# Two expert blocks of the second mixture layer moved in front of its last routing step, and one choice for the last two sequences

## The chip, the cores and the metric

The kernel runs on one core of a Trainium2 chip. A core has a matrix engine (TensorE, written PE, with its weight loads as PEld), a vector engine (VectorE, DVE), a scalar engine (ScalarE, ACT), a general engine (GpSimd, POOL) and a synchronising engine (SyncE, SP), which issues most transfers. The metric is the time on the device in microseconds (us), lower is better. Everything is computed in float32.

## The reference

The input is 2048 tokens of 128 numbers, as 8 sequences of 256 tokens for the attention. Each of the six sub-layers is added to the stream x:

```python
x = x + 0.5 * ffn(layernorm(x))          # mixture of experts, "layer 1"
x = x + attention(layernorm(x))          # 16 heads of 8, softmax
x = x + 0.5 * ffn(layernorm(x))          # same weights, "layer 2"
x = x + 0.5 * channel_mix(layernorm(x))
x = x + gated_conv(layernorm(x))
x = x + 0.5 * channel_mix(layernorm(x))
```

The mixture of experts has 8 experts, of which each token takes the two with the largest logits:

```python
h = rmsnorm(s @ W_in.T, in_norm_w)                    # 128 -> 128
logits = h @ Wr.T                                     # 8 experts
_, idx = top_k(logits + expert_bias, 2)
gates = softmax(the two logits)
for e in range(8):
    oe = rmsnorm(silu(h @ Wg[e].T) * (h @ Wu[e].T) @ Wd[e].T, enorm_w[e])   # hidden 512
    out = out + gates[:, e] * oe
return rmsnorm(out, out_norm_w) @ W_out.T
```

## The kernel before, in words

A tile is 128 tokens; x is held as four chunks of four tiles. The two mixture layers don't compute all experts for all tokens: each token's row is written to the two places in device memory where the rows of its experts are collected, and the experts then work on blocks of such rows.

`dispatch` (line 338) is the routing for one part of the tiles. Its steps are: `turned` and `measured` (transpose x and take its statistics), `product` (the router's and the input projection, PE, `pin`), `summed` and `inverted` (1/rms: `ri`), `scaled` (the row that is sent, `hrow`, two ACT copies for a tile), `logits`, `choice` twice (first and second expert), `ranked` and `placed` (the row's place among its expert's rows: two products `prank`, and the sums of the tiles before in `ahead`), and `rows` (line 465), two indirect transfers from POOL for a tile, into `hs`. For layer 2 the tiles are cut by `LATE` (line 59) into parts of 4, 4, 4, 2 and 2 tiles. In the first three of layer 2 the 1/rms is POOL's power function (`power_of`, line 170); in layer 1 and in the last two parts of layer 2 it is ACT's square root (line 398) and DVE's reciprocal (line 405).

`counts` (line 492) then has PE sum how many rows each expert has (`pcnt`), and `table` (line 564) works out on DVE, in seven steps (`counted`, `summed`, `paired`, `spared`, `singled`, `named`, `bounded`), which expert and which rows each block takes.

`experts` (line 679) works through blocks. Blocks 24 to 31 are early blocks, one of 128 rows for each expert, whose places are known without the table: their rows are among those of the first tiles (6 tiles in layer 1, 8 in layer 2, `LEAD`) and are read ahead by `leading` (line 517), which also fetches their weights. The others are led by the table: pairs of 256 rows and singles of 128 (numbers 15 and up), in the order of `TURNS` (line 48). For each block i, `work` (line 782) issues: `gate(i)` (eight or four-by-two products `pg`, and ACT's Silu into `sg`), `turn_rows(i+1)` (`pht`, `ht`), `up(i)` (`pu`, and DVE's product `hg`), one step of the table, and `down(i-1)` (`py`, the row's sum of squares `ysq` on ACT, the product with the norm's weights on DVE, two index operations, and one indirect transfer from POOL into `y` for each 128 rows). `py` has one bank of PSUM, so a block's `py` waits until DVE has read the last one. After the last block, `combine` (line 807) reads `y` and adds the two experts of each token.

PE, DVE, ACT and SP execute in the order in which the program issues; POOL's indirect transfers are held in program order too. Attention is a pipeline of steps, and `at(s, h, ...)` puts pieces of layer 2's routing into half-steps of it (lines 1240 to 1300). The last lines of that list bring the last sequences, the rows 0 to 3 of the third part, and the two parts of two tiles each (names ending in 6 and 7, tiles 12 and 13, 14 and 15):

```python
at(33, "a", lead["read"], u6, places, partial(rows, [0]))
at(33, "b", root_table, s6, partial(rows, [1]), w(2))
at(34, "a", partial(turn_back, b), partial(rows, [2]), w(4), i6, l6, c6[0])
at(34, "a", partial(turn_heads, b), partial(rows, [3]), w(2), h6, partial(out_heads, b))
at(34, "a", w(2), x7, w(2), m7, c6[1], u7, w(2), s7, r6)
at(34, "a", i7, p6, rows6, l7, *c7, h7, r7, p7, rows7)
```

`turn_back`, `turn_heads` and `out_heads` are the end of attention for a sequence (`pot`, `pcc`, `ct`, `pwo`, and the addition to x); `w(n)` are n products without use which keep PE busy; `root_table` loads ACT's square root ahead of its use. The expert blocks begin after all of this, in `second_experts` (line 937).

Of the kernel before, what the change touches and what calls it, by code (L numbers as in the profile page):

```python
# [2 lines left out]

# [13 lines left out]
P = 128  # L17
# [28 lines left out]
LEAD = 6, 8  # L46
LEADING = list(range(NT, NT + E))
TURNS = (
    [0, 1, 2, 15, 3, 4, 5, 16, 6, 7, 8, 17, 9, 10, 18, 11],
    [0, 1, 2, 15, 3, 4, 5, 6, 16, 7, 8, 9, 17, 10, 11, 12],  # L50
# [6 lines left out]
EARLY = (0, 4), (4, 4), (8, 4), (12, 4)  # L57
LATE = (0, 4), (4, 4), (8, 4), (12, 2), (14, 2)
# [15 lines left out]
def macaron_kernel(ctx: ExitStack, tc: tile.TileContext, a: dict, out: bass.AP):  # L74
# [70 lines left out]

    root_table()

# [190 lines left out]
    def dispatch(f, i, parts, mp):  # L338
# [5 lines left out]
        paced = f == 1 and i < len(parts) - 2  # L344
# [4 lines left out]
        def turned():  # L349
            pt = bank(f"pxt_{n}", "sa")  # L350
            for t in range(nt):
                nc.tensor.transpose(pt[:, ts(t, P)], x[:, t, :], ident)
            st["xt"] = xntp.tile([P, CT], F32, tag="xnt", name=f"xnt_{n}")
            nc.scalar.copy(st["xt"][:, 0 : nt * P], pt[:, 0 : nt * P])
            st["u"] = mp.tile([P, TPC, D + E], F32, tag="u", name=f"u_{n}")[:, 0:nt]
            st["ss"] = small.tile([P, nt], F32, tag="ss", name=f"ss_{n}")

        def measured():
            bs = small.tile([P, nt, 6], F32, tag="ast", name=f"ast_{n}")
            mv = small.tile([P, nt, 2], F32, tag="amv", name=f"amv_{n}")  # L360
            for t in range(nt):
                nc.vector.bn_stats(bs[:, t, :], x[:, t, :])
            for t in range(nt):
                nc.vector.bn_aggr(mv[:, t, :], bs[:, t, :])
            st["z"] = small.tile([P, nt], F32, tag="z", name=f"z_{n}")
            nc.vector.tensor_scalar(st["z"], mv[:, :, 1], RMS_EPS, RMS_EPS * LN_EPS, ALU.mult, ALU.add)
# [25 lines left out]
        def summed():  # L392
            ri = small.tile([P, nt], F32, tag="ri", name=f"ri_{n}")
            nc.vector.scalar_tensor_tensor(ri, st["ss"], 1.0 / D, st["z"], ALU.mult, ALU.add)
            if f == 0:
                nc.vector.tensor_copy(hrow[:, :, :, D].bitcast(I32), tokid[:, slots])
            if f == 0 or i >= len(parts) - 2:
                nc.scalar.activation(ri, ri, AF.Sqrt)
            else:
                power_of(ri, ri, mhalf.to_broadcast([P, nt]))  # L400
            st["ri"] = ri

        def inverted():
            if f == 0 or i >= len(parts) - 2:
                nc.vector.reciprocal(st["ri"], st["ri"])
# [59 lines left out]
        def rows(ts_=range(nt)):  # L465
            for t in ts_:
                if paced:
                    nc.vector.tensor_copy(st["posi"][:, t, :], st["pos"][:, t, :])
                for k in range(2):
# [5 lines left out]
                    )  # L475
                    tc.declare_no_dep(ins.ins, group=f"hs{f}", reason="rows of their own")
# [11 lines left out]
        if i < len(parts) - 2:  # L488
            return turned, *halves, measured, summed, logits, scaled, *choices, both(ranked, placed), rows
        return turned, halves[0], measured, summed, inverted, logits, scaled, *choices, ranked, placed, rows  # L490

    def counts(f):
        pc = bank(f"pcnt_{f}", "sb")[:, 0:E]
# [22 lines left out]

    def leading(f, gp, homes, rows, yrows):
# [6 lines left out]
        lead["taken"], lead["base"], lead["masks"], lead["idx"] = flags[:, 0], flags[:, 1], masks, idx  # L524

# [19 lines left out]

        def read():
# [5 lines left out]
            for e, row in enumerate(first):  # L552
                hst = rows[e].unsqueeze(1)
# [7 lines left out]
        lead.update(weights=weights, flagged=flagged, read=read)  # L561
# [117 lines left out]
    def experts(f, tab, far, y2, mp, pieces, lead):  # L679
# [3 lines left out]
        hst, w = lead["hst"], lead["w"]  # L683

# [3 lines left out]
        def fetch_weights(t):  # L688
# [3 lines left out]
            e = nc.values_load(tab[0:1, 1, t : t + 1], engines=[SP], min_val=0, max_val=E - 1)  # L692
# [47 lines left out]
        def down(t):  # L740
# [27 lines left out]
            for s in range(m):  # L768
# [10 lines left out]
                if t >= NT:  # L779
                    tc.keep_in_program_order(ins)  # L780
# [961 lines left out]
```

## Time and profile before

| what | us |
|---|---|
| median of three runs (lowest, highest) | 590.76 (589.77, 591.71) |
| the profiled execution's own time | 588.57 |
| its span | 586.8 |
| PE busy | 512.5 (87%) |
| DVE busy | 357.2 (61%) |
| ACT busy | 277.7 (47%) |
| POOL busy | 194.1 (33%) |
| chain that ended last: PE, ACT, DVE, DMA | 64%, 11%, 11%, 9% |
| mean granted PE clock | 0.954 of full speed |

The span holds, one after the other: layer 1's routing (to about 41 us), its early blocks and table blocks (to 154), its combination and the attention (to 354), the end of attention with layer 2's routing of the last tiles and its early blocks (354 to 394), layer 2's table blocks (to 479), and the tail. A row of the timeline gives the start, the busy time, the engine, the line, the operation and its operands, and in square brackets how long the engine stood idle before it and whose work ended the wait. A row of windows gives a stretch with its length and the busy time of each engine in it (with the number of instructions), then the mean clock that PE was granted, the busy share of the DMA engines and the rate in GB/s. In the chain of waits a piece has a start, a length and what it is.

### The profile page before, as it was taken

Reading aid. Unit: us, or ns where it says so; the run is one execution under the profiler, and the core shown is the slowest. Engines: PE = TensorE matmul, PEld = TensorE weight load, DVE = VectorE, ACT = ScalarE, POOL = GpSimd, SP = SyncE. Lnnn points to the kernel's source line nnn. Section 1 sums busy time; section 2 is a strip of 40 time slices with the busy share of each in tenths; the row PEclk is TensorE's granted clock in tenths of the full one; section 3 lists DMA queues with packets and bytes.
Section 4 is the critical chain, followed back from the end, with each engine's and each line's share of the span. In section 5 each row is a group of like instructions: output and inputs, shape, how many; then the busy total and the mean of one; then the engine's idle time right before and its main releaser. Section 6 shows DMA issues by size and latency. Waiting matters only on the chain.

```text
span 586.8 us, 11358 instructions
## 1 busy us (share of the span) xinstructions
PE 512.5 (87%) x3954; PEld 398.6 (68%) x3954; DVE 357.2 (61%) x1129; ACT 277.7 (47%) x683; POOL 194.1 (33%) x202
## 2 busy tenths in 40 slices
PE   5459799999779989998898886989999978799996
PEld 5349788899546555565465554989999945478884
DVE  5777464564336667767768876664444424758775
ACT  4564223222234556566756654433332316874275
POOL 0677546753331201011003356532342335410200
PEclk9559999999989999999999999899999989989998
DMA  8933846765041264073063017455776514000002
GB/s 305 377 91 124 286 159 217 219 185 186 21 109 32 42 165 198 2 203 160 24 127 113 26 36 242 168 173 193 222 224 217 156 45 123 1 1 1 1 0 73
DMA packets 37952, 76.96 MB, mean 131 GB/s; under 512 B 4667, under 2 KB 27106, under 8 KB 36608
## 3 DMA queue, kind: packets, MB, share of 16 engines
q1 hardware_dynamic: 33360, 66.62, 36.3%
q0 software_dynamic: 4528, 9.52, 4.5%
q8 instruction: 35, 0.57, 0.4%
q14 instruction: 29, 0.24, 0.1%
HBM read 55.28 MB, written 21.44 MB: 131 GB/s over the span
## 4 chain that ended last, share of the span: by engine, by line
PE 64%; ACT 11%; DVE 11%; DMA 9%; issue 3%; POOL 1%; SPq 0%; DVEq 0%; ACTq 0%; POOLq 0%
PE pg_f L722 10%; PE pu_f L722 10%; PE ps L1127 9%; PE py_f L745 8%; DMA y<-yrow_f,idx_f 5%; ACT es L1164 4%; PE po L1174 3%; PE pvf L1496 2%; PE pgo L1523 2%; DMA qk<-heads 2%; PE pm L1110 2%; DVE m L1147 2%; PE pin_f L374 1%; PE pk_m L1440 1%; PE pht_f L709 1%
## 5 line engine op out<-in xcount | busy, mean ns | idle before, releaser
L1164 ACT ACTIVATE es<-ps 128x1024 f32<-128x1024 f32 x64 | 65.3, 1021 | 52.9 <-PE ps L1127 31.2
L1147 DVE TENSOR_REDUCE m<-pm 128x4 f32<-128x1024 f32 x64 | 77.4, 1220 | 12.8 <-PE pm L1110 12.7
L1127 PE MATMUL ps<-qa,qk 32*128 32x256 f32 x512 | 73.0, 401 | 11.8 <-ACT es L1164 9.5
L769 POOL DMA_INDIRECT y<-yrow_f,idx_f x57 | 56.0, 983 | 79.3 <-issue 44.3
L470 POOL DMA_INDIRECT hs<-hrow,posi_f x64 | 61.7, 964 | 53.7 <-issue 19.3
L738 DVE TENSOR_TENSOR hg_f<-pu_f,sg_f 128x1024 f32<-128x1024 f32 (+1 forms) x48 | 46.5, 968 | 48.7 <-PE pu_f L722 48.6
L1110 PE MATMUL pm<-qk 32*128 32x256 f32 x512 | 73.8, 401 | 0.9 <-ACT qk L1057 0.6
L762 ACT ACTIVATE ysq_f<-py_f 128x128 f32<-128x128 f32 x73 | 19.7, 274 | 100.2 <-PE py_f L745 91.4
L1127 PEld LDWEIGHTS ps<-qa,qk 32*128 32x128 f32 x512 | 43.6, 184 | 29.7 <-ACT es L1164 22.1
L731 ACT ACTIVATE sg_f<-pg_f 128x1024 f32<-128x1024 f32 (+1 forms) x48 | 39.3, 819 | 44.3 <-PE pg_f L722 42.7
L745 PE MATMUL py_f<-w_f,hg_f 128*128 128x128 f32 x456 | 56.7, 277 | 2.0 <-DVE yrow_f L763 2.0
L745 PEld LDWEIGHTS py_f<-w_f,hg_f 128*128 128x128 f32 x456 | 54.9, 192 | 3.6 <-DVE yrow_f L763 2.3
L722 PE MATMUL pg_f<-ht_f,w_f 128*128 128x256 f32 (+1 forms) x256 | 54.7, 357 | 0.0
L722 PE MATMUL pu_f<-ht_f,w_f 128*128 128x256 f32 (+1 forms) x256 | 54.7, 357 | 0.0
L1110 PEld LDWEIGHTS pm<-qk 32*128 32x128 f32 x512 | 44.6, 184 | 3.3 <-issue 1.5
L722 PEld LDWEIGHTS pu_f<-ht_f,w_f 128*128 128x128 f32 x256 | 43.1, 191 | 4.4
L722 PEld LDWEIGHTS pg_f<-ht_f,w_f 128*128 128x128 f32 x256 | 43.0, 191 | 3.8
L171 POOL TENSOR_TENSOR cf_f<-cf_f,mhalf 128x8 f32<-128x8 f32 (+1 forms) x9 | 13.5, 1503 | 65.8 <-DVE cf_f L834 64.2
L1174 PE MATMUL po<-es,v 128*32 128x256 f32 x512 | 34.3, 385 | 0.0
L763 DVE TENSOR_TENSOR yrow_f<-py_f,w_f 128x256 f32<-128x256 f32 (+1 forms) x32 | 12.7, 396 | 34.6 <-ACT ysq_f L762 32.0
L1159 DVE TENSOR_TENSOR qa<-pmt,qk 128x256 f32<-128x256 f32 x32 | 13.5, 422 | 25.7 <-PE pmt L1153 25.6
L714 DVE TENSOR_SCALAR ht_f<-pht_f,pack 128x256 f32<-128x256 f32 (+1 forms) x32 | 14.5, 453 | 17.3 <-PE pht_f L709 17.3
(327 smaller groups left out, 982.8 us busy)
## 6 DMA issues: line engine op xcount, KB each, us to landing
w_f<-in_wall_dram SPq DMA_DIRECT2D x32, 832.0 KB, 4.6
hs<-blank SPq DMA_DIRECT2D x8, 1032.0 KB, 15.1
qk<-in_wall_dram SPq DMA_DIRECT2D x7, 832.0 KB, 6.5
w_lead<-in_wall_dram SPq DMA_DIRECT2D x7, 832.0 KB, 12.5
y_f<-y SPq DMA_DIRECT2D x14, 258.0 KB, 3.1
hst_f<-hs SPq DMA_DIRECT2D x25, 129.0 KB, 2.2
pack<-in_pack_dram SPq DMA_DIRECT2D x1, 1729.0 KB, 8.5
v<-in_wall_dram SPq DMA_DIRECT2D x2, 832.0 KB
```

Source lines behind the costliest of these rows:

```text
L470: ins = nc.gpsimd.indirect_dma_start(out=hss[f], out_offset=bass.IndirectOffsetOnAxis(ap=st["posi"][:, t, k : k + 1], axis=0), in_=hrow[:, ...
L722: nc.tensor.matmul(ph[:, k, :], w[t][:, o + k * P : o + k * P + P], ht[t], start=True, stop=True)
L731: nc.scalar.activation(sg, pg, AF.Silu)
L738: nc.vector.tensor_mul(hg[t], pu, sg)
L745: nc.tensor.matmul(py[:, s, :], hg[t][:, k, ts(s, P)], w[t][:, 2 * DFF + k * D : 2 * DFF + k * D + D], start=(k == 0), stop=(k == NFC - 1),)
L762: nc.scalar.activation(sq[:, s], py[:, s], AF.Square, accum_out=yrow[:, s, D : D + 1])
L769: ins = nc.gpsimd.indirect_dma_start(out=y2, out_offset=bass.IndirectOffsetOnAxis(ap=idx[:, s : s + 1], axis=0), in_=yrow[:, s, :], in_off ...
L1110: nc.tensor.matmul(sc[:, jj, i, :], qs[c][r, g, col + i * P : col + (i + 1) * P], ks[c][r, g, col : col + S], start=True, stop=True,)
L1127: nc.tensor.matmul(sc[:, jj, i, :], ks[c][r, g, col + i * P : col + (i + 1) * P], tops[s][r, :], start=True, stop=True,)
L1147: nc.vector.tensor_reduce(m, sc, AX.X, ALU.max, negate=True)
L1164: nc.scalar.activation(es, sc, AF.Exp, scale=scale)
L1174: nc.tensor.matmul(po[32 * j : 32 * j + 32, :], vs[c][:, (b % 2) * 2 + i, (g % 2) * (H // 2) + (g // 2) * 4 + j, :], ess[s, j // 2][:, j % ...
```

## The change

- `LATE` and `EARLY` become one `PARTS` of four tiles each: the last two sequences (tiles 12 to 15) are transposed, measured, multiplied and scaled two tiles at a time, but they have one `logits`, one `choice`, one `ranked`, `placed` and `rows`. Their 1/rms goes to POOL's power function, and `silu_table` stands where `root_table` stood in layer 2.
- The blocks 24 and 25 (`BEGUN = 2`) are issued from attention's list, between and behind the steps of that last part: transpositions, gate and up products ahead of and around the routing's `prank`, with smaller tiles of attention's pool and banks of their own; their y rows are sent after the last routing row. `second_experts` begins with block 26.
- The table begins in that list as well: `counts` (now in the bank `sa`), `counted` and `summed`. The remaining steps are spread over the blocks: one for each block in layer 1, with `bounded` in a block of its own; two for each in layer 2.
- In layer 1 the weights of all eight early blocks are asked for at the start (seven before); y rows of the early blocks and the table's scratch move to other buffers. For the first table block the weights are asked for ahead of the rows.
- The index operations of the eight early blocks are done once for all (`numbers`), and for the other blocks ahead of the product with the norm's weights.
- `TURNS`: in layer 1 the single 18 comes after the pair 11, in layer 2 the single 17 after the pair 12.

```diff
-    [0, 1, 2, 15, 3, 4, 5, 16, 6, 7, 8, 17, 9, 10, 18, 11],
-    [0, 1, 2, 15, 3, 4, 5, 6, 16, 7, 8, 9, 17, 10, 11, 12],
+    [0, 1, 2, 15, 3, 4, 5, 16, 6, 7, 8, 17, 9, 10, 11, 18],
+    [0, 1, 2, 15, 3, 4, 5, 6, 16, 7, 8, 9, 10, 11, 12, 17],
...
-EARLY = (0, 4), (4, 4), (8, 4), (12, 4)
-LATE = (0, 4), (4, 4), (8, 4), (12, 2), (14, 2)
+PARTS = (0, 4), (4, 4), (8, 4), (12, 4)
...
-        paced = f == 1 and i < len(parts) - 2
+        paced = f == 1 and i < len(parts) - 1
...
-            if f == 0 or i >= len(parts) - 2:
+            if f == 0:
                 nc.scalar.activation(ri, ri, AF.Sqrt)
             else:
-                power_of(ri, ri, mhalf.to_broadcast([P, nt]))
+                power_of(ri, ri, mhalf.to_broadcast([P, hi - lo]))
...
+    def number(out, rows, keep, set_):
+        nc.vector.tensor_tensor(out, rows[:, :, D].bitcast(I32), keep, ALU.bitwise_and)
+        nc.vector.tensor_tensor(out, out, set_, ALU.bitwise_or)
...
+        def numbers():
+            o = 0
+            for ap, n in rows:
+                got = ap.rearrange("p (e r) -> p e r", r=ROW)
+                number(idx[:, o : o + n], got, masks[:, 0, o : o + n], masks[:, 1, o : o + n])
+                o += n
...
         def up(t, sg):
             pu = hidden(t, "pu", DFF)
+            if lead["small"]:
+                hg[t] = sg
...
+            def ask(upto, i):
+                nonlocal asked
+                while asked < min(upto, n) and (turns[asked] >= NT or i >= ready):
+                    first = turns[asked] == TURNS[f][0]
+                    for fetch in (fetch_weights, fetch_rows) if first else (fetch_rows, fetch_weights):
+                        fetch(turns[asked])
+                    asked += 1
...
+    def begin_table(f, pc, gp, lead, scratch):
+        lead["tab"], lead["far"], lead["steps"] = table(f, pc, gp, lead, scratch)
+        lead["steps"].pop(0)()
+
+    def run_experts(f, gp, lead, turns, pieces):
+        m, steps = len(turns), lead["steps"]
+        k = -(-len(steps) // (m - 2))
+        steps = [both(*steps[o : o + k]) for o in range(0, len(steps), k)]
+        ready = len(steps) - 1
+        steps += [lambda: None] * (m - len(steps))
+        lead["tiles"].work(turns + TURNS[f], steps + pieces, ready)
...
-            for e in range(7):
+            for e in range(E):
                 lead["weights"](e)
...
-                at(33, "b", root_table, s6, partial(rows, [1]), w(2))
-                at(34, "a", partial(turn_back, b), partial(rows, [2]), w(4), i6, l6, c6[0])
-                at(34, "a", partial(turn_heads, b), partial(rows, [3]), w(2), h6, partial(out_heads, b))
-                at(34, "a", w(2), x7, w(2), m7, c6[1], u7, w(2), s7, r6)
-                at(34, "a", i7, p6, rows6, l7, *c7, h7, r7, p7, rows7)
+                at(33, "b", s6, partial(rows, [1]), w(2), silu_table)
                 at(34, "a", *(partial(lead["weights"], e) for e in (3, 4, 5)))
+                at(34, "a", partial(turn_back, b), w(4), partial(rows, [2]), h6)
+                at(34, "a", partial(turn_heads, b), w(2), partial(out_heads, b), w(2), x7, w(2), m7, u7)
+                at(34, "a", T(0), s7, partial(rows, [3]), G(0), T(1), l67, G(1), c67[0], U(0), c67[1])
+                at(34, "a", r67, h7, p67, rows67, counted, U(1), summed, Y(0), Y(1), send_begun)
```

Here `T`, `G`, `U` and `Y` stand for `turn_rows`, `gate`, `up` and `down` of an early block, `l67` to `rows67` for the steps of the last part, `h6` and `h7` for its rows' copies of two tiles each.

## The prediction

> **What bounds the kernel now.** The busy times come first: TensorE (PE) 512.5 us of the span of 586.8 us, VectorE (DVE) 357.2, ScalarE (ACT) 277.7, GpSimd (POOL) 194.1; the chain that ended last is 64% PE. So a change pays only where PE stands idle, and the change touches four such places. The windows around layer 2's beginning show the first (columns: the stretch, then busy time and count of PE, weight loads, DVE, ACT, POOL, then the granted clock).
>
> ```profile
> 354.00:360.50 6.50, 6.03 (x28) 3.23 (x27) 4.63 (x25) 4.02 (x9) 4.71 (x5) 1.00 0.71 165
> 360.50:365.60 5.10, 0.76 (x4) 0.60 (x4) 3.71 (x24) 1.80 (x7) 3.88 (x5) 0.97 0.99 388
> 365.60:369.70 4.10, 3.61 (x15) 3.32 (x16) 2.30 (x13) 1.65 (x2) 2.89 (x4) 0.50 1.02 418
> 369.70:372.70 3.00, 3.00 (x19) 3.00 (x18) 0.73 (x2) 0.85 (x2) 2.38 (x3) 0.59 0.81 309
> ```
>
> PE works 0.76 us in 5.1, and the next 7 us run at half clock. The timeline says what PE waits for there:
>
> ```profile
> 356.67 0.37 ACT L1087 COPY ct<-pcc 128x256 f32<-128x256 f32 x1 [0.55 <-PE pcc L1085]
> 356.94 0.91 ACT L414 ACTIVATE hrow<-u_f,ri_f 128x256 f32<-128x256 f32 x2
> 357.09 0.96 POOL L470 DMA_INDIRECT hs<-hrow,posi_f  x1 [0.30 <-ACT ct L1087]
> ...
> 365.63 0.61 PE L442 MATMUL prank_f<-mask_f,pack 128*128 128x16 f32 x2 [3.70 <-DVE mask_f L435]
> 366.93 0.47 PE L709 MATMUL pht_f<-ident,m 128*128 128x128 f32 x1
> 367.83 1.28 ACT L731 ACT_TABLE_LOAD   x1
> 367.86 2.08 PE L722 MATMUL pg_f<-ht_f,qk 128*128 128x128 f32 x8 [0.46 <-ACT ht_f L712]
> 369.98 0.60 ACT L731 ACTIVATE sg_f<-pg_f 128x512 f32<-128x512 f32 x1 [0.86 <-PE pg_f L722]
> 374.68 1.06 PE L722 MATMUL pg_f<-ht_f,v 128*128 128x128 f32 x8
> ```
>
> The choice of the last two tiles (mask, L435) holds PE; the first expert's block starts at 366.93 and its gate product takes 2.08 us, against 1.06 for the same eight matmuls at 374.68. Layer 1's beginning has two stalls inside its early blocks:
>
> ```profile
> 59.63 1.16 PE L745 MATMUL py_f<-w_lead,hg_f 128*128 128x128 f32 x8 [1.51 <-DVE lidx L766]
> 62.56 0.35 SPq L695 DMA_DIRECT2D w_f<-in_wall_dram  x1
> 65.61 1.13 PE L722 MATMUL pg_f<-ht_f,w_lead 128*128 128x128 f32 x8 [2.03 <-DMA w_lead<-in_wall_dram]
> 68.58 0.63 PE L722 MATMUL pg_f<-ht_f,w_f 128*128 128x256 f32 x2
> ```
>
> 1.51 us go to the table on DVE (named and bounded, 56.05 to 59.3, ahead of the block's output), 2.03 us to the eighth expert's weights, issued only at 59.64. And the ends of both layers' block lists stand in the chain as one transfer each, the scatters of the y rows:
>
> ```profile
> 144.27 16.06 DMA y<-yrow_f,idx_f
> ```
>
> ```profile
> 468.60 13.02 DMA y<-yrow_f,idx_f
> ```
>
> The y read begins only when the last scatter has landed: last scatter at 156.08, read at 160.41; in layer 2, 478.35 and 481.75. An end's time is the start of its last scatter.
>
> **Ends (order of turns).** Layer 1 now runs 10, 11, 18, single 18 last, instead of 10, 18, 11; layer 2 11, 12, 17 instead of 17, 10, 11, 12. In layer 1 the last up product ends at T = 148.78 whichever is last. Before: py_18 at T, py_11 at 150.61 after a wait of 0.78 for the one output bank, scatters 154.80 and 156.08. After: py_11 at T. From a pair's output start to its first scatter took 4.19 us (472.88 to 477.07); the index operations, now ahead of the product with the row weights, take about 0.25 off: T+3.94, second T+5.22, single's T+6.50 (pitch 1.28, its row ready at T + 3.12 + 2.54 = T+5.66). 155.28 against 156.08: -0.8 us. Layer 2: one output pair (1.95) rather than a single (1.05) is done before T, so T moves from 469.76 to 470.66; last scatter 477.16 against 478.35: -1.2 us. Sum -2.0; bounds -2.6 (the scatter's issue gap before 154.80 falls away) and -1.2.
>
> **Layer 1's beginning.** All eight weights are asked for at the start. The extra 832 KB take 2.0 us at the 420 GB/s which the DMA moves there; it is saturated until about 27 us, the rows are read at 34.03, the first block's transposition is at 40.61: hidden, and if not, at most 2.0 us late. The 2.03 wait goes. The table's steps are spread one to a block, with bounded in a block of its own, so the 1.51 wait goes too, to at most 0.4 of a remainder. What is late next: w_f for the first table block, now ahead of its rows in SP's queue, waits for the fifth early expert's buffer (about 61.0) and lands 4.6 us later (the issue row's median) or 5.8 (the eighth's weights above), 65.6 to 66.8; the rows queue behind it, issued about 62.2, landed 2.2 to 3.4 later. Without waits the first table block's gate product would come at 68.58 - 3.54 = 65.0, so it comes at 66.9 to 68.1 (landing, turn 0.4, copy 0.5, and the early block's rest). I take 67.4: -1.2 us; ends -1.7 and -0.5. The indices for all eight early blocks at once take 12 to 16 operations of 0.15 us from DVE per layer; PE doesn't wait for DVE there, so nothing.
>
> **Layer 2's beginning.** Three parts. *(a) The 1/rms of tiles 12 and 13 goes from ACT's root and DVE's reciprocal to POOL's power.* POOL sends scatters in order every 1.26 us (354.57, 355.83, 357.09): the power stands behind two of them, so 356.79, and takes 0.70 (the nearest row is the 128x2 power, 725 ns): 357.49. ACT's order now has the two hrow copies (0.91) ahead of ct. ct came at 356.67 before; now 357.55 + 0.87 = 358.42. Behind ct stand pwo, x, pxt, xnt, pin, u: all +1.75, so pin 361.1 to 361.8, the squares to 363.0. Cost +1.75, between 0.5 (power one scatter earlier) and 3.0 (one later).
> *(b) Blocks 24 and 25.* After pin: ht_24 363.3, pg_24 363.3 to 364.4, pg_25 to 366.4, pu_24 to 367.4, all ahead of prank. DVE is in order: logits after POOL's power of tiles 14 and 15 (363.2 to 363.9; its four scatters end by 362.5, slack 0.7), six choice operations of 128x32 at a pitch of 0.22 to 365.7, then hg_24, which waits for pu_24: 367.5 to 368.2, and the second half of the choice (five operations and the mask) behind it: 369.5; ahead x4, both, lsel, at_row: 370.9. pcnt, in the same bank as prank, 371.1 to 371.5; pu_25 to 372.6, py_24 to 373.6. Counts, hg_25, the summed step, index operations and m_24 to 375.7 hold py_25 (one output bank): 375.75 to 376.8; two ACT operations of block 26 and pg_26 at 377.7. Before, pg_26 stood at 374.68 with py_25's 1.06 still to do: 375.74. So +2.0.
> *(c) Spread table steps:* the wait of 1.51 at 385.11 becomes 1.05: -0.5. Sum for layer 2's beginning: **+1.5 us**; bounds -0.6 (ct unheld) and +4 or more (below).
>
> Two rules bear on (b). The clock: above, 4.7 us of idle PE gave half clock. The Trainium skill (TensorE: Matmul & The Clock Gate, Part 1: The HAM clock gate) says that the clock halves after an idle window of some 3.4 us, and needs as long a busy one to return. After, no gap that I find is over 2.1 us (367.4 to 369.5), so by the rule PE stays warm, and my matmuls have 1.06. But the rule watches busy share, and no row here shows a stretch of PE a third busy: at half clock each of the six groups takes 1.0 more. The table: the Silu load (1.28 us at 367.83) goes to where the root's was, one load fewer. The skill (ScalarE: Activation LUTs, What ACT_TABLE_LOAD costs) has 1.38 us of drain beside 1.28, which credits 2.66 here. The row has sg_24 at 369.98, 0.04 after pg_24's end: load and drain were hidden or absent. I credit nothing.
>
> **Sum.** Ends -2.0, layer 1's beginning -1.2, layer 2's +1.5: -1.7. The profiled execution took 588.57 (span 586.8, 1.8 around it), which becomes 586.9; the median of the three runs is 590.76 (589.77 to 591.71), 2.2 above the profiled one, and a difference carries over: **589.1 us**. A measurement of this kernel tells about 0.3% (1.8 us) from no change: faster is below 588.99, slower above 592.53. The likeliest case lies at that edge.
>
> **Rivals.**
> *It goes as forecast*, 587.6 to 590.8: 0.42; 0.2 of it below 588.99.
> *A: the clock falls in layer 2's beginning.* PE has from 361.8 to 375 some 6 us of work in 13, and if the gate takes that for idle, pg_24, pg_25, pu_24 come 3 us later, hg_24 and the choice with them, then pu_25, py_24 and py_25 add 1 each with part of it beside DVE: +4.8, so 593.9, and 596 where the power of tiles 14 and 15 comes late too. It decides from about 3.4 us, four of six groups cold. For it: 0.50 in the row above. Against: the gaps under 3.4. With the unseen waits which a new order brings, 0.28.
> *B: ct is hardly held and layer 1 gains in full*: POOL's power fits in one scatter earlier. +0.3 - 1.7 - 2.0 = -3.4: 587.4, down to 585.5 with all lower bounds. For it: POOL idles 3.23 us before 354.57. Against: the order of scatters is fixed. 0.18.
> *C: layer 1's gain is eaten*: w_f and its rows land late (5.8 and 3.4) or the start is late by 1 to 2 us. 590.5: 0.12. The change then does nothing measurable.
> Faster: 0.20 + 0.17 = 0.37. Slower: A, 0.28, and 0.02 from C. Same: 0.33. Range 586.0 to 594.5: it leaves out 0.06 below and 0.12 above. The likeliest case alone: 587.6 to 590.8.
>
> **What would show it.** Right: ct after two hrow copies at about 358.4; the first block's gate product at about 363.3 with eight matmuls in 1.06; pg_26 at about 377.7; the clock at 1.00 from 361 to 378; no idle time before the eighth block's gate product in layer 1, and pg_0 at about 67.4; last scatters 6.5 us after the last up product in both layers. Wrong: a clock of 0.5 in that stretch (A); a wait on POOL's power of tiles 14 and 15; pg_0 at 68.5 or later (C); blocks starting after 41.5 in layer 1; or a changed pace of attention, where I expect none.

## The result: slower, by 1.2%

| | before | after |
|---|---|---|
| median of 13 runs, us | 589.98 (588.34 to 592.78) | 599.07 (592.46 to 602.08) |
| ratio | 1 | 1.0121 (95%: 1.009 to 1.0153) |
| profiled execution, us | 588.57 | 601.58 |
| its span, us | 586.8 | 599.8 |
| granted PE clock, mean | 0.954 | 0.932 |

The ratio leaves out runs that took over 1.5% longer than the fastest of their kernel, three of after's 13 and its profiled one among them, and isn't the quotient of the medians, which is 1.0154. The forecast of 589.1 was wrong, and so was its range, which ended at 594.5. The profiled execution of after lies near the top of its runs, 13.0 us over that of before, where the medians differ by 9.1. So the trace shows where the time went, and the experiments, which have many runs, say how much each place is worth.

The runs of the changed kernel also have a mean granted clock each. Two at 0.950 and 0.951 took 592.46 and 593.13 us, seven at 0.936 to 0.939 took 597.95 to 599.39, three at 0.929 to 0.932 took 601.39 to 602.08; only the last one, at 0.974 with 596.37, is out of line. So executions of one program lie up to 9.6 us apart, and the time goes with the clock.

### Where the 13 us are

The same landmarks in both traces (us from the start of the span; in brackets the time since the landmark before):

| landmark | before | after | difference that arises here |
|---|---|---|---|
| first table block's Silu, layer 1 | 70.55 | 75.58 | +5.0 (forecast -1.2) |
| first exponential of attention | 185.31 (114.8) | 190.33 (114.8) | 0.0 (forecast -0.8) |
| last exponential of attention | 350.87 (165.6) | 356.29 (166.0) | +0.4 (forecast 0) |
| first table block's Silu, layer 2 | 395.23 (44.4) | 408.87 (52.6) | +8.2 (forecast +1.5) |
| end of the span | 586.8 (191.6) | 599.8 (190.9) | -0.6 (forecast -1.2) |

A second execution of after (after_3, 601.68 us, from a later group of runs) has the same picture: 75.33 at the first landmark, and 53.4 us for layer 2's beginning.

The head of the page for after:

```profile
span 599.8 us, 11288 instructions
PE 522.5 (87%) x3948; PEld 407.9 (68%) x3948; DVE 350.9 (58%) x1081; ACT 276.3 (46%) x680; POOL 195.8 (33%) x204
```

PE's busy time rose from 512.5 to 522.5 us, with 3948 matmuls where before had 3954. VectorE has less to do than before (350.9 against 357.2). So PE was busy 10.0 us longer for about the same work: its clock was lower.

**Layer 1's beginning.** The timeline of after, PE, SP's queue and DVE's last reading of the fifth block, at the first table block (start, busy time, engine, what, and the wait before it):

```profile
62.48 0.28 DVE L807 TENSOR_TENSOR m<-py_f,w_lead 128x128 f32<-128x128 f32 x1
62.91 0.33 SPq L733 DMA_DIRECT2D w_f<-in_wall_dram  x1
64.53 1.59 SPq L741 DMA_DIRECT2D hst_f<-hs  x2
69.11 0.69 PE L747 MATMUL pht_f<-ident,hst_f 128*128 128x128 f32 x2 [4.25 <-DMA hst_f<-hs]
69.59 1.92 PE L761 MATMUL pu_f<-ht_f,w_lead 128*128 128x128 f32 x8
71.30 1.92 PE L787 MATMUL py_f<-w_lead,hg_f 128*128 128x128 f32 x8
73.00 2.54 PE L761 MATMUL pg_f<-ht_f,w_f 128*128 128x256 f32 x8
```

The blocks don't start late: the first one's transposition comes at 40.83, before at 40.61. The old stalls of 1.51 and 2.03 us are gone, as forecast. In their place stands one of 4.25: the table block's rows (`hst_f`) were issued at 64.53 behind its weights (`w_f`) and landed at 69.1. PE then ran at half clock: 1.92 where before it took 1.06, 2.54 where it took 1.93.

**Layer 2's beginning.** The timeline of after, where the choice and the first early blocks lie:

```profile
362.23 0.73 POOL L176 TENSOR_TENSOR ri_f<-ri_f,mhalf 128x2 f32<-128x2 f32 x1
363.00 0.91 ACT L422 ACTIVATE hrow<-u_f,ri_f 128x256 f32<-128x256 f32 x2 [1.55 <-POOL ri_f L176]
363.81 0.35 ACT L1154 COPY ct<-pcc 128x256 f32<-128x256 f32 x1
...
369.60 1.16 PE L761 MATMUL pg_f<-ht_f,qk 128*128 128x128 f32 x8 [1.35 <-ACT ht_f L750]
371.70 2.08 PE L761 MATMUL pg_f<-ht_f,qk 128*128 128x128 f32 x8 [0.84 <-ACT ht_f L750]
377.24 0.41 PE L450 MATMUL prank_f<-mask_f,pack 128*128 128x32 f32 x2 [2.07 <-DVE mask_f L443]
379.00 2.05 PE L761 MATMUL pu_f<-ht_f,qk 128*128 128x128 f32 x8
380.85 1.91 PE L787 MATMUL py_f<-qk,sg_f 128*128 128x128 f32 x8
384.05 2.08 PE L787 MATMUL py_f<-qk,sg_f 128*128 128x128 f32 x8 [1.28 <-DVE m L807]
386.84 2.08 PE L761 MATMUL pg_f<-ht_f,v 128*128 128x128 f32 x8 [0.50 <-ACT ht_f L750]
```

The long wait of 3.70 for the choice has become one of 2.07 with the two blocks around it. But five of the six groups of eight matmuls shown take about 2 us where 1.06 is possible. The windows of after over this stretch (busy time and count of PE, weight loads, DVE, ACT, POOL, then the clock) show how little work came before and between:

```profile
364.00:369.00 5.00, 4.04 (x15) 3.08 (x15) 1.31 (x6) 1.32 (x6) 3.06 (x4) 0.66 0.95 312
369.00:374.00 5.00, 3.56 (x19) 3.33 (x20) 1.76 (x10) 1.58 (x7) 2.72 (x3) 0.73 1.03 410
374.00:379.00 5.00, 2.45 (x13) 2.02 (x13) 3.32 (x16) 1.21 (x3) 0.00 (x0) 0.84 0.54 216
379.00:384.00 5.00, 3.76 (x17) 3.47 (x17) 3.80 (x18) 0.37 (x2) 3.10 (x4) 0.50 0.08 26
384.00:389.00 5.00, 4.45 (x19) 4.05 (x20) 0.29 (x1) 0.67 (x4) 3.79 (x4) 0.50 0.16 53
```

In windows of 1 us the clock falls three times: at 364 (behind the hold of `ct`, where PE was busy for 0.49 of the two microseconds before), at 371, and at 378, where it stays at 0.50 until 391.

**The ends.** In the chain of waits of before, each layer's scatters stood as one piece. Of after that view covers only 17% of the span, so timelines stand here: layer 1's end before, then after, and then the last scatter of layer 2 after:

```profile
155.27 1.74 PE L197 MATMUL warm_f<-pack,ident 128*128 128x512 f32 x4 [2.60 <-DVEq L804]
157.01 2.05 PE L290 MATMUL ptf<-filt,pack 128*128 128x128 f32 x16
166.04 0.62 PE L854 MATMUL pan_f<-ident,acc_f 128*128 128x128 f32 x2 [2.50 <-DVE acc_f L845]
```

```profile
158.92 0.97 POOL L812 DMA_INDIRECT y<-yrow_f,idx_f  x1 [0.31 <-issue]
160.93 3.33 PE L202 MATMUL warm_f<-pack,ident 128*128 128x512 f32 x4 [3.62 <-DVE filt L289]
164.05 3.11 PE L295 MATMUL ptf<-filt,pack 128*128 128x128 f32 x16
167.94 3.70 PE L202 MATMUL warm_y<-pack,ident 128*128 128x512 f32 x8 [0.78 <-DVE tf L298]
171.48 0.38 PE L908 MATMUL pan_f<-ident,acc_f 128*128 128x128 f32 x2
...
490.21 0.98 POOL L812 DMA_INDIRECT y<-yrow_f,idx_f  x1 [0.30 <-DVEq L856]
```

In layer 1 the last up product ends at T = 153.02 (where the output product behind it starts), and the last scatter starts at 158.92, T + 5.90; the read of y follows at T + 10.31, where before it came at T + 11.63. Yet attention gained nothing: PE reaches the first product of the combination (`pan_f`) at 171.48 without a wait, because fillers and the filter's transpositions stand ahead of it on PE. PE had been idle for 3.62 ahead of them, 2.60 before, and they ran at the lower clock: the four fillers took 3.33 against 1.74, the transpositions 3.11 against 2.05, together 2.65 more. Before, `pan_f` had waited 2.50 for its sum at 166.04. The wait was exchanged for PE's own queue.

### The profile page after: what moved, and what is told of

It reads as the page before. It is cut to its first block, busy times and chain, and to the rows that moved or that the text cites. A ratio compares the mean times of both kernels' runs of the same rounds, so it can differ in the third digit from the quotient of the medians.

```text
span 599.8 us, 11288 instructions
## 1 busy us (share of the span) xinstructions
PE 522.5 (87%) x3948; PEld 407.9 (68%) x3948; DVE 350.9 (58%) x1081; ACT 276.3 (46%) x680; POOL 195.8 (33%) x204
## 5 line engine op out<-in xcount | busy, mean ns | idle before, releaser
L779 DVE TENSOR_TENSOR hg_f<-pu_f,sg_f 128x1024 f32<-128x1024 f32 (+1 forms) x46 | 45.1, 980 | 51.5 <-PE pu_f L761 51.5
```

The costliest lines, as they stand in the source:

```text
L779: nc.vector.tensor_mul(hg[t], pu, sg)
```

## Experiments

Theory 1: the loss in layer 1 is the order of weights and rows on SP's queue. Rival: the granted clock fell there for some other reason, or the earlier request of all weights delayed the start. Theory 2: in layer 2 the hold of `ct` costs 1.75, and the half clock the rest. Rival: the two moved blocks cost their time at any clock. The ratios are to the kernel before in the same group of runs, with 95% intervals.

### Each part by itself

Rows ahead of weights for the first table block:

```diff
-                    for fetch in (fetch_weights, fetch_rows) if first else (fetch_rows, fetch_weights):
+                    for fetch in (fetch_rows, fetch_weights):
```

> The changed kernel, with the rows of layer 1's first table block asked for ahead of its weights again. In the changed kernel the weights' transfer waits for an early block's buffer (issued 62.91) and the rows stand behind it (64.53, landed 69.1); PE idles 4.25 us, then runs at half clock, and the first table block's Silu is 5.03 us later than before. Theory (the queue order is the cause): rows issued by 61.5, no idle of over 1 us before their transposition, that Silu at or before 70.5, and the whole 4.5 to 6.5 us under the changed kernel, about 592. Rival (the rows land late because the DMA is busy with weights and scatters, whatever the order): they land 4 us or more after their issue, the gain is under 2 us, about 597.

The rows' copies that hold `ct`, moved one step back:

```diff
-                at(34, "a", partial(turn_back, b), w(4), partial(rows, [2]), h6)
-                at(34, "a", partial(turn_heads, b), w(2), partial(out_heads, b), w(2), x7, w(2), m7, u7)
+                at(34, "a", partial(turn_back, b), w(4), partial(rows, [2]))
+                at(34, "a", partial(turn_heads, b), w(2), h6, partial(out_heads, b), w(2), x7, w(2), m7, u7)
```

> The changed kernel, with the two hrow copies of tiles 12 and 13 issued after the copy ct of attention's last sequence instead of ahead of it. Theory (the hold of ct starts the loss: PE idles, its clock falls): ct about 1.7 us earlier, PE's clock stays at full speed until the first gate product, and block 26's Silu comes 4 to 6 us earlier: the whole about 594. Rival (the clock falls anyway because PE has little to do between the choice's steps): only the 1.7 us come back, about 597.4, and the clock in the stretch stays under 0.8.

Fillers where PE has little to do (`v(n)` are n useless products in a bank of their own):

```diff
+                at(34, "a", partial(turn_heads, b), w(6), partial(out_heads, b), w(2), x7, w(2), m7, u7)
+                at(34, "a", T(0), v(4), s7, partial(rows, [3]), G(0), T(1), v(2), l67, G(1), c67[0], U(0), v(6), c67[1])
```

> The changed kernel, with more products without use on PE in layer 2's beginning: 6 instead of 2 ahead of pwo, 4 after the first block's transposition, 2 after the second's, 6 ahead of the last part's rank product. Theory (half clock is the largest term of layer 2's loss): clock over 0.9 in the stretch from attention's last output to block 26, the six products of blocks 24 and 25 at about 1.06 us each, block 26's Silu 3 to 5 us earlier, the whole about 595. Rival (the order of DVE and POOL sets the pace there): the clock is full, but the Silu moves by less than 1.5 us, about 598.

The kernel before with the new `TURNS` alone:

> The kernel before, with only the order of the last table blocks changed: a single last in both layers (10, 11, 18 and 11, 12, 17). Theory of the prediction without the earlier index operations: last scatter at 6.75 us after the last up product, -0.5 in layer 1 and -1.0 in layer 2: about 588.5 where the kernel before has 590. Rival (what is gained at the scatter is lost again in the combination, on PE's clock or on the landing of y): within 0.5 us of the kernel before although the scatters are earlier.

On the chip of this group the kernel before took 619.12. Measured: rows_first 0.9956 (0.993 to 0.9983), h6_late 1.0014 (0.9992 to 1.0037), warm 1.0014 (0.9991 to 1.0037), turns 1.0016 (0.9994 to 1.0039). The traces say what each edit did in its place. rows_first took 4.8 to 6 us out of layer 1's beginning, measured from the eighth early block. In h6_late `ct` came 5.80 us after the last exponential instead of 7.52, so the hold is 1.72. In warm the fillers held the clock for a while, yet layer 2's beginning was no shorter (51.4 us, against 51.2 in after_again below, on another such chip): the clock was 1.00 until about 398 and six products took 1.06 to 1.16; then one wait of 2.47 for the one output bank followed a thin stretch, and it was half gone again (windows of warm):

```profile
398.00:403.00 5.00, 2.35 (x12) 1.96 (x13) 2.21 (x11) 0.70 (x4) 3.83 (x4) 0.78 0.16 53
403.00:408.00 5.00, 5.00 (x27) 5.00 (x27) 0.00 (x0) 0.85 (x2) 3.87 (x4) 0.54 0.16 53
```

In turns the last scatter of layer 1 came at T + 6.63 instead of T + 7.30, and nothing was gained at the end. This chip has waits of its own that no kernel here accounts for; the profile calls them remote. The waits of DVE in turns show one such line:

```profile
DVE hg_f L738 <- remote: 14.0, 1, 14.0
```

ACT has one of 11.03 in the same stretch and one of 6.68 in layer 2's beginning. Against the trace of before, turns is 23.2 us later at layer 1's first table block, and its layer 2's beginning is 7.5 us longer. That second place is just where the change works, so what it costs there can be partly hidden. No trace here shows what causes these waits.

### The edits together, on a second such chip

The changed kernel again:

> The changed kernel itself, as the control beside the three that follow, since chips differ by some per cent. All theories: 0.9 to 1.5% slower than the kernel before where transfers are as quick as in the first result; where the start is longer by waits for transfers, between equal and 0.5% slower.

rows_h6 is the changed kernel with both edits, rows_first and h6_late:

> The changed kernel with the rows of layer 1's first table block ahead of its weights, and with the hrow copies of tiles 12 and 13 behind ct. If the two losses add: 5 us less by the rows and 2 us less by the copies, 7 us under the changed kernel in the same call (about 0.988 of it), close to the kernel before. If the hold of ct costs nothing once PE's clock has fallen anyway: 5 us less.

rows_h6_begun0 moves the two early blocks back out of attention's list:

```diff
-BEGUN = 2
+BEGUN = 0
...
-                at(34, "a", T(0), s7, partial(rows, [3]), G(0), T(1), l67, G(1), c67[0], U(0), c67[1])
-                at(34, "a", r67, h7, p67, rows67, counted, U(1), summed, Y(0), Y(1), send_begun)
+                at(34, "a", s7, partial(rows, [3]), l67, *c67)
+                at(34, "a", r67, h7, p67, rows67, counted, summed)
```

> As rows_h6, but no early block is moved: blocks 24 and 25 begin behind the last rank product again, everything else stays (one choice for four tiles, table begun early). Theory (moving the blocks costs, because they split the choice on DVE and PE runs them at half clock): layer 2's beginning, from the last exponential to the first table block's Silu, takes 2 to 5 us less than in rows_h6, and the whole is that much faster. Rival (the moved blocks fill time in which PE would idle, and the loss is the common choice's and POOL's power): 2 to 5 us slower than rows_h6.

rows_h6_fill adds fillers to rows_h6 and takes block 24's output ahead of `summed`:

> As rows_h6, with products without use on PE between the early blocks' steps (4, 2, 6 and 6) and block 24's output ahead of the table's second step on DVE. Theory (half clock, and the output held behind the table, are what is left of layer 2's loss): clock over 0.95 from attention's last output to block 27, no product of blocks 24 to 27 over 1.3 us, layer 2's beginning 4 to 6 us shorter than in rows_h6, and the whole 4 to 6 us faster: 5 us under the kernel before. Rival (DVE's and POOL's order sets the pace at any clock): under 2 us.

Here before took 617.97. Measured: after_again 1.004 (1.0022 to 1.0058), rows_h6 0.9894 (0.9846 to 0.9943), rows_h6_begun0 0.9896 (0.9843 to 0.9948), rows_h6_fill 0.9942 (0.9919 to 0.9965). The two edits are worth 9 us together; the moved blocks cost nothing that shows here. rows_h6_fill was slower than rows_h6 by the medians (614.64 against 612.25; the intervals just overlap): DVE idled for 7.46 us ahead of one `hg_f`, the last 3.7 of them with both inputs written, and the trace names no cause. The changed kernel lost only 0.4% here; on chips with before near 590 it loses more. The runs below are from such chips.

### On chips where before takes 589

> The changed kernel once more as the control of this call. If [...]: 1.0 to 1.4% slower than before. If not (before at about 618): 0.2 to 0.6% slower, since the kernel before then loses 6 us of its own in layer 2's beginning.

> The changed kernel with both undone orders (rows ahead of weights; hrow copies behind ct), again. Whatever the chip, 7 to 8.5 us under the changed kernel of this call if the two are what makes the change slow; on a chip where before takes 590 us this is then equal to before within 1.5 us. If a chip [...]gives the moved blocks' own cost room to show, only 5 us under the changed kernel and 2 to 3 us slower than before.

> As rows_h6, with no early block moved, again. In the third call the two were equal (612.4 and 612.3). If that equality is the moved blocks' real value: within 1 us of rows_h6. [...]on a chip where before takes 590 us, 2 to 5 us faster than rows_h6 (the moved blocks cost), or 2 to 4 us slower (they gain).

rows_h6 with the old `TURNS`, so that a difference to rows_h6_2 is the turns:

> As rows_h6, with the order of the last table blocks of the kernel before (pair last). Theory (the earlier last scatter is lost again, since PE's products without use and the filter's transform stand ahead of the combination's first product): within 0.7 us of rows_h6. Rival (the prediction's 2.0 us are real): 1.5 to 2.5 us slower than rows_h6.

Before 589.3. Measured: after_3 1.0185 (1.0156 to 1.0214), rows_h6_2 1.0008 (0.9986 to 1.003), begun0_2 0.9941 (0.9919 to 0.9964), rows_h6_oldturns 1.0018 (0.9997 to 1.0039). So the two edits remove 10.4 of the 10.9 us. The timeline of rows_h6_2 in layer 1 shows the rows issued at 60.35, ahead of the weights, and PE at full clock:

```profile
60.35 0.38 SPq L741 DMA_DIRECT2D hst_f<-hs  x1
62.10 0.35 SPq L733 DMA_DIRECT2D w_f<-in_wall_dram  x1
63.81 0.38 PE L747 MATMUL pht_f<-ident,hst_f 128*128 128x128 f32 x2
67.47 1.96 PE L761 MATMUL pg_f<-ht_f,w_f 128*128 128x256 f32 x8 [1.50 <-DMA w_f<-in_wall_dram]
```

The first table block's gate product comes at 67.47, and the Silu at 69.48, 1.07 earlier than in before: this is the gain that the prediction had put there, but now by the other order. The first exponential comes at 182.95, 2.36 earlier than in before.

The pair rows_h6_2 and rows_h6_oldturns gave more than was asked of it. In layer 2's beginning the two programs are the same; they differ in the turns of the table blocks alone. Their windows there, first rows_h6_2:

```profile
360.00:366.00 6.00, 2.90 (x23) 2.36 (x22) 3.92 (x20) 2.24 (x5) 2.91 (x4) 1.00 1.00 381
366.00:372.00 6.00, 4.17 (x20) 3.86 (x20) 4.71 (x23) 0.37 (x2) 3.10 (x4) 0.72 0.59 236
372.00:378.00 6.00, 5.27 (x43) 4.90 (x44) 2.00 (x8) 2.19 (x7) 4.56 (x5) 1.00 0.17 55
```

then rows_h6_oldturns:

```profile
360.00:366.00 6.00, 3.09 (x25) 2.66 (x24) 3.47 (x17) 2.25 (x5) 3.44 (x4) 0.98 1.01 404
366.00:372.00 6.00, 5.23 (x22) 4.70 (x22) 4.58 (x21) 0.37 (x2) 2.66 (x3) 0.50 0.60 239
372.00:378.00 6.00, 4.69 (x20) 4.30 (x21) 0.97 (x6) 0.92 (x4) 4.48 (x6) 0.50 0.13 44
```

PE is half busy in both up to 366. In the one the clock comes back by 372, in the other it stays at 0.50, and layer 2's beginning lasts 45.63 against 50.24 us. So this stretch lies at the edge at which the clock is granted, and one kernel can fall on either side. That the spread of the timed runs (rows_h6_2: 586.79 to 592.67) is this is likely: its four runs with a mean clock of 0.939 to 0.942 took 589.58 to 592.67, the six at 0.950 and above 586.79 to 589.88. But only the profiled executions show a clock for the stretch. The profiled rows_h6_2 is the fastest of its twelve runs, 3.0 us under their median.

What the moved blocks cost at full clock can be read from this trace and that of begun0_2, on the same chip. PE's waits there, first two lines of rows_h6_2, then the one long wait of begun0_2:

```profile
372.12 1.16 PE L787 MATMUL py_f<-qk,sg_f 128*128 128x128 f32 x8 [1.68 <-DVE m L807]
382.74 1.16 PE L787 MATMUL py_f<-qk,hg_f 128*128 128x128 f32 x8 [1.69 <-DVE m L807]
```

```profile
363.86 0.61 PE L450 MATMUL prank_f<-mask_f,pack 128*128 128x32 f32 x2 [6.64 <-DVE mask_f L443]
```

With the blocks in the gap, DVE does `hg_24` in the middle of the choice, and the rank product comes 16.75 us after the last exponential, in begun0_2 15.73. The first product of block 26 comes no earlier (25.49 against 25.14), and the wait of 1.69 for DVE, which has the table's steps ahead, is still there (1.51 in before), where begun0_2 has none. Layer 2's beginning lasts 45.63 us, against 44.11 in begun0_2, where the first blocks run at half clock.

### One edit and fillers, and a better kernel

> The changed kernel with the rows of layer 1's first table block ahead of its weights, nothing else, on another chip than in the second call. If layer 1's loss is the queue order: 6 to 7 us under the changed kernel by the trace up to attention's first exponential (190.0 to 183), so on a chip where before takes 590 us about 594.5, 1.007 to 1.009 of before. The rest is layer 2's.

rows_warm is rows_first with the fillers of warm; rows_h6_warm2 is rows_h6 with `v(4)`, `v(2)` and `v(6)`:

> As rows_first, with products without use on PE: 6 instead of 2 ahead of pwo, 4, 2 and 6 between the steps of blocks 24 and 25 and ahead of the rank product. Clock theory (the hold costs its 1.7 us, half clock the rest): layer 2's beginning, last exponential to the first table block's Silu, falls from about 52.5 to 47.5 us, and the whole by 4 to 5 us. Rival (the order of DVE and POOL sets the pace): under 1.5 us. If the clock falls all the same behind block 24's output, where nothing fills: about half.

> As rows_h6 (hrow copies behind ct), with the same products without use except the 6 ahead of pwo. rows_h6 took 45.6 us in this stretch with the clock high and 50.2 in a twin with the clock low. Clock theory: always near 45.5, the median 2 us under rows_h6's (0.997 of before), and the runs closer together. Rival: the products delay the early blocks as much as they win; within 1 us of rows_h6's 1.001.

The kernel of the next run is rows_h6_begun0 unchanged, in spite of its label:

> The version without moved blocks once more, one look beside the others, for its ratio on this chip: 0.992 to 0.996 where before takes 590 us, 0.989 where it takes 618.

Before 589.13. Measured: rows_first_2 1.0044 (1.0024 to 1.0065), rows_warm 1.0023 (0.9991 to 1.0054), rows_h6_warm2 0.999 (0.9974 to 1.0007), begun0_warm one execution of 587.79. The fillers bring 1.2 us to rows_first and 1.1 to rows_h6 (against rows_h6_2), both within the intervals. They don't bring the 4.6 us by which the two executions above differ: they are PE time themselves, and in both profiles the clock falls to 0.50 again behind them. The twenty runs of rows_h6_warm2 do lie closer together (587.10 to 590.71).

Last, rows_h6_begun0 again and with 24 fillers while the choice runs:

```diff
-                at(34, "a", s7, partial(rows, [3]), l67, *c67)
+                at(34, "a", v(24), s7, partial(rows, [3]), l67, *c67)
```

> The changed kernel with rows ahead of weights, hrow copies behind ct and no early block moved. On a chip where before takes 590 us: 0.992 to 0.996 of before, as in the fourth call (0.9941 from 4 runs).

> The same with 24 products without use (5.1 us of PE at full clock) between the last tiles' router product and their rank product, where PE otherwise idles about 6.6 us. Clock theory: no product of block 24 and 25 over 1.3 us, layer 2's beginning 2 us shorter (44 to 42 us), the whole 2 us under begun0_3. Rival: the pace there is set by DVE's and ACT's part of the blocks, under 0.7 us.

Before 588.78. Measured: begun0_3 0.9951 (0.9923 to 0.998), median 586.02; begun0_filled 0.9934 (0.9913 to 0.9956), median 584.76. Both beat the kernel before and the changed one; between the two the intervals overlap, and layer 2's beginning is 0.7 us shorter with the fillers (43.73 against 44.40), not 2. In the windows of begun0_filled the fillers end at 364.06, and the next 4.3 us were thin enough to lose the clock for the first blocks:

```profile
364.00:368.30 4.30, 1.56 (x8) 1.03 (x7) 3.72 (x22) 0.37 (x1) 0.86 (x2) 0.96 1.02 421
368.30:371.00 2.70, 2.67 (x12) 2.67 (x13) 1.37 (x6) 0.56 (x2) 2.09 (x3) 0.50 0.72 282
```

### What each part is worth

From the ratios on the chips with before near 590, times 589. The runs after_3, rows_h6_2, begun0_2 and rows_h6_oldturns are from one chip, rows_first_2 and begun0_3 from another, so a row that takes from both also holds what the two chips differ by:

| part | from | us |
|---|---|---|
| weights ahead of rows, layer 1 | after_3 1.0185 less rows_first_2 1.0044 | 8.3 |
| the same, with the first result | 1.0121 less rows_first_2 1.0044 | 4.5 |
| hold of `ct` | rows_first_2 1.0044 less rows_h6_2 1.0008 | 2.1 |
| everything else in the change | rows_h6_2 1.0008 | 0.5 |
| of this: the two moved blocks | rows_h6_2 less begun0_2 (3.9), less begun0_3 (3.4) | 3.4 to 3.9 |
| of this: the turns | rows_h6_oldturns 1.0018 less rows_h6_2 1.0008 | -0.6 |

The rows for the order of weights and for the moved blocks stand clear of the intervals; the other three do not, though the trace shows the 1.72 of `ct` directly. The changed kernel itself measured 1.0121 and 1.0185, and these two intervals don't overlap; so a difference between groups of runs can be wrong by some 4 us, and the first part is worth 4.5 to 8.3. For the turns the medians, 591.80 and 589.79, differ by 2.0 where the ratios differ by 0.6; in the traces the two ends together differ by 0.5.

## Why the prediction was wrong, by its steps

Two steps failed, and they are two of the rivals, A and C, which had been priced as alternatives and came together. In the profiled execution layer 1's beginning missed its forecast by 6.2 us and layer 2's by 6.7.

**Layer 1's beginning, "I take 67.4: -1.2 us", failed: the gate product came at 73.00.** That the weights stand ahead of the rows on SP's queue was seen, and priced at an arrival of the rows between 64.4 and 65.6. Three terms were too small. The buffer that `w_f` waits for came free at 62.76, not 61.0, since it is freed by DVE's last reading of the fifth block, which stands behind the table's steps; so the rows were issued at 64.53, not 62.2. They took 4.6 us, not 2.2 to 3.4, behind the weights. And PE is in order: the eighth block's up and output products stand behind the table block's transposition, so 4.25 us idle came first, and these and the gate product then ran at half clock: 0.86 + 0.86 + 0.6, a cost that the sum didn't have. The ratios say 4.5 to 8.3 us for this order against a gain of 1.2 in the sum; at this place the traces show 4.2 (after against rows_first_2, whose Silu comes at 71.40 since its gate product waits 2.38 for the weights and then takes 3.37) to 6.1 (against rows_h6_2), and 4.8 to 7.4 by the first exponential. Of the 9.0 us between the traces of after and rows_first_2, 4.8 arise up to there and 3.6 from layer 2's beginning on, where the two programs are the same; whether the order has a part in these stays open. The rival named *layer 1's gain is eaten* was this mechanism, priced at 1.4 us (590.5 against 589.1). The part of the step that speaks of the two old stalls was right: both went.

**Layer 2's beginning (a), the hold of `ct`, was right.** Forecast 358.42 in before's time, which with the 5.42 us of delay up to the last exponential is 363.84; measured 363.81. Undoing it moved `ct` by 1.72 (forecast 1.75).

**(b), the two blocks, was right in its steps and wrong in the clock.** In rows_h6_2, without the hold and with two of the six groups at half clock for the most part, `pg_26` comes at 374.00, 25.49 after the last exponential; the prediction's steps without the hold give 377.7 - 1.75 - 350.87 = 25.1. In after it comes at 386.84, 30.55 after, 3.7 later than the forecast: the six groups before it (`pg_24` to `py_25`) took 0.1 + 1.0 + 0.5 + 1.0 + 0.9 + 1.0 = 4.5 over 1.06 each, part of it beside DVE. The three groups from `pg_26` on took 2.08, 1.92 and 1.59, 2.4 more. With the 1.5 of the forecast and the 0.5 of (c) that didn't come, this is the 8.2 of the table but for 0.1. It is rival A, whose price was 4.8. The step that failed is "after, no gap that I find is over 2.1 us, so by the rule PE stays warm". The gaps were right (the largest is 2.07), the conclusion was not. The Trainium skill (TensorE: Matmul & The Clock Gate, Part 1: The HAM clock gate) speaks of an idle window of some 3.4 us; here PE was busy for 2.45 of 5.0 us in pieces, and the groups behind it ran at 0.50. Here a stretch was sparse enough without one long gap, and the measurement decides over the rule as I had read it. The "4.7 us of idle PE" of the forecast were in truth two gaps of 0.58 and 3.70 with 0.40 of work between, so even that row didn't show that it takes one long gap. The sentence that the gate watches busy share should have moved the chance of A up.

And the cost of the blocks isn't the clock alone: in rows_h6_2's profile, with the clock mostly full, the stretch was still 1.5 us longer than in begun0_2. In begun0_3 they stand behind the choice again, and their first product takes 2.08 at half clock as in before, and yet this kernel is 3.4 us faster than rows_h6_2. The forecast of +2.0 for (a) and (b) together, of which 1.75 is (a), left 0.25 for moving them; the ratios say 3.4 to 3.9, in which rows_h6_2's runs at a lower clock may have a share. The step had put `hg_24` into the choice on DVE, and (c) had the table's wait shrink; neither sum says that begun0_2's order, with all blocks behind the choice, would hide that wait altogether.

**(c), -0.5 for the spread table steps, isn't there.** The wait that was to shrink from 1.51 to 1.05 is 1.46, and the two Silus around it stand 4.51 apart, before 4.57.

**The ends, -2.0, failed though the scatters came as forecast or better**: T + 5.90 in layer 1 and T + 5.91 in layer 2 (490.21 less 484.30), forecast T + 6.50. In layer 1 the wait that this shortens was already shared with PE's own queue, and the work in that queue fell to the lower clock, so the first exponential gained nothing. (In rows_h6_2 and begun0_2, with the same turns, this stage is 1.2 to 1.3 us shorter than in before, in begun0_3 0.2 longer; in rows_h6_oldturns, with the old turns, it is 1.3 shorter too, so the turns don't decide it.) From layer 2's table blocks to the end 0.6 us was gained instead of 1.2. The turns alone measure 0.6 us in rows_h6, within the intervals, and none in the kernel before. I had made the start of the last scatter the end's time without asking what PE does meanwhile.

**What was held to be nothing.** The requests for all weights at the start, the indices for all early blocks and the table's load were costed at nothing. What remains of the change in begun0_2, with the two edits and without the moved blocks, is 3.5 us faster than before, so together they cost nothing that shows; they weren't tried one by one.

What stays open: the waits called remote on the chips where before takes 618, why the changed kernel measured 1.0121 in one group and 1.0185 in another, and why rows_h6_fill lost time with inputs ready. None was tried.

## To carry to other kernels

In a queue that issues in order, a request that must wait for a buffer also holds what stands behind it: give the small transfer that is needed first its place ahead, and ask when the buffer really comes free, not when its product is done. When work is moved into a gap of PE, count how much of the whole stretch is busy, not the longest gap, and price each product behind it at both clocks; then follow the engine that PE had waited for, which may now have more ahead of what PE needs. A shortened wait is a gain only if the engine that waited has nothing else queued ahead of it.

## What the runs showed of the hardware

PE at 2.45 of 5.0 us busy, with no gap over 2.07, was followed by more than ten microseconds at half clock; 1.56 of 4.3 by at least 2.7. The same instructions (rows_h6_2 and rows_h6_oldturns) were granted 1.00 in one execution and 0.50 in another six microseconds long at 372, and the stretch differed by 4.6 us. Over the whole span, runs of one program at a mean clock of 0.950 took 592.5 us and at 0.929 602.1. Two chips took 618 to 619 us for a kernel that takes 589 to 590 on the others, and there the change cost 0.4%, where it cost 1.85% on one of the others.
